# A recurrent token-mixing block on one core: zero matmuls ahead of the first transposes, the first batch's scaled rows taken from SBUF, and another written order

## The chip, the cores and the metric

The kernel runs on one core of one Trainium2 chip. Its engines work side by side, each on a queue of its own that it takes strictly in order: PE (TensorE, matrix products into PSUM), DVE (VectorE), ACT (ScalarE), POOL (GpSimd), and SP (SyncE), which here only issues DMAs. The metric is the device time of one execution in microseconds (us). Three runs of the kernel before took 615.41, 615.86 and 616.64 us; the median is 615.86 us.

## What is computed

One block of a recurrent network (RWKV-like) over x of shape 8 batches x 256 tokens x 512 channels, in float32, cut to what matters:

```python
xn = ln(x, ln1_w, ln1_b);  sx = shift(xn) - xn             # shift: the token before
xxx = tanh((xn + sx * maa_x) @ maa_w1).reshape(b, l, 5, 1, 32)
x5 = xn[:, :, None] + sx[:, :, None] * (maa_stack + xxx @ maa_w2)   # five mixes of each token
w = exp(-exp(time_decay + tanh(x5[:, :, 1] @ decay_w1) @ decay_w2))
r, k, v = x5[:, :, 3] @ Wr.T, x5[:, :, 0] @ Wk.T, x5[:, :, 2] @ Wv.T
g = silu(x5[:, :, 4] @ Wg.T)
# per head (32 heads of 16), token by token:
out = r @ (u * outer(k, v) + s);  s = outer(k, v) + w * s
att = groupnorm(out) * gn_w + gn_b
x = x + (att * g) @ Wo.T
xn2 = ln(x, ln2_w, ln2_b);  sx2 = shift(xn2) - xn2
x = x + sigmoid((xn2 + sx2*maa_r) @ Wr2.T) * (square(relu((xn2 + sx2*maa_k) @ Wk2.T)) @ Wv2.T)
```

## The kernel before

**Layout.** Between the two layer norms the activations lie with channels on the partitions: 512 channels are four blocks of 128, held as two tiles q = 0, 1 of two blocks m = 0, 1 each, with 256 tokens along the free axis. `normed` takes the statistics of the rows as they come from HBM (tokens on the partitions), scales them to `xh`, and `turned` turns them with eight transposes on PE (line 588) into PSUM tiles `ps`, from which `xn` is written with the norm's weight and bias.

**Stages.** For each of the 8 batches there are three: `inputs_of_scan` (norm, the mix `xin` with its product by `maa_w1` and the tanh `ta`, the products with `maa_w2`, called the psm products below, the five mixes `x5`, the decay, and the projections k, v, r, g), `scan`, and `rest` (group norm, output product, second norm, feed-forward). The stages of neighbouring batches run interleaved. The scan of a batch has 16 pieces: v is written to HBM as `vo` and read back in a spread layout as `vs`; DVE multiplies it by k (line 883), runs the recurrence with a scan instruction whose decay `wrep` lies in PSUM (line 885); POOL multiplies by r (line 888); PE sums over partitions (`gather`, line 896), four gathers a batch, 32 in all.

**The written order.** Every instruction group is an `Op` in a `Plan`. `TURNS` is a long string of numbers, one rank for each op and one list for each stage. `Plan.order` goes through the ops by rank, gives out buffers from the pools, computes a start for each op with a small model (`us` is an op's planned length), sorts by that start, and emits the instructions in that order. So ranks decide the order on every queue, which buffer a tile gets, and where an ACT function table has to be loaded again. `Plan.tiles` also decides from that order whether a product goes to PE as one 128-column matmul or as four of 32 columns that run side by side (`narrow` in `mul`, line 398); both take PE the same time. In the trace each float32 matmul is two records, a transpose one.

**The start.** Only for batch 0, `normed(..., alone=True, first=early)` is used: DVE does the statistics (line 554), ACT one square root (line 557), DVE the reciprocal and `xh` (lines 559 and 562). Then, for each block, two instructions read the same PSUM tile: DVE writes `xn` (line 595) and ACT writes the mix tile (line 598) as `ps * ow0 + ow1`. `owners` (line 517) prepares those two factors on POOL in four small instructions: ow0 = ln1_w (1 - maa_x) and ow1 = ln1_b (1 - maa_x). DVE then adds the shifted row times maa_x (line 622), POOL forms `sx` (line 610), and PE multiplies `xin` by `maa_w1`; between the transposes and these products PE has the `centered_weights` products (128x128, 16 of them) that subtract each head's mean from the v weights. `head_masks` (line 528) are four small DVE instructions that fill `hm`, needed later by the scan.

**The end.** The last batch's `rest` ends with the products `fk`, `fr`, `fv`; `fr` goes through a sigmoid on ACT (line 986), and the last token tile is written out in two halves.

Of the kernel before, what the change touches and what calls it, by code (L numbers as in the profile page):

```python
# [67 lines left out]
class Plan:  # L68
# [46 lines left out]
    def stage(self):  # L115
# [225 lines left out]
def tile_rwkv_block(  # L341
# [73 lines left out]
    dw1, dw2 = const("dw1", [P, NK, DEC]), const("dw2", [2 * DEC, E])  # L415
    hm = const("hm", [P, NK, 32])
    eh = const("eh", [P, 4])
    ow = const("ow", [P, 2, NK])
    W = {n: [const(f"W{n}{h}", [P, 2, E]) for h in range(2)] for n in "kvrg"}

    pool("s0", 2, [P, NK, S])
# [95 lines left out]
    def owners():  # L517
        i, j = (VECS.index(v) for v in ("maa_x", "ln1_w"))
        for n in range(2):
            gp(4, ow, [vec], lambda n=n: nc.gpsimd.tensor_tensor(  # L520
                ow()[:, n, :], vec()[:, :, j + n], vec()[:, :, i], ALU.mult), 30)
# [593 lines left out]
```

## Time and profile before

| what | value |
|---|---|
| median of three runs | 615.86 us (615.41 to 616.64) |
| the profiled execution's own time | 616.02 us |
| its span, first to last instruction | 614.2 us |
| matmul records in it | 7068 |
| HBM traffic | 115.25 MB read, 8.39 MB written |
| granted TensorE clock | 1.000 |

All durations below come from this one profiled execution. A row of the timeline has start and length in us, the engine, the line, the operation, the tiles, and in brackets how long the engine sat idle before it and what ended that. A row of the chain of waits has start, length, engine, tile and line; following the rows in order shows what the end of the span hung on at each time. A row of the table by stretches has the stretch, its length, and then the busy time of PE, PE's weight loads, DVE, ACT and POOL, with instruction counts. A busy PE row covers pipelined matmuls whose ends are modelled, so busy is not the same as full speed.

### The profile page before, as it was taken

How to read it: one execution, taken by the hardware profiler on the slowest of the kernel's cores; microseconds unless marked ns; L12 is line 12 of the kernel's file. 1: busy time of each engine (PE TensorE's matmuls, PEld its weight loads, DVE VectorE, ACT ScalarE, POOL GpSimd, SP SyncE). 2: the span in 40 equal slices, each digit the busy share in tenths (PEclk: the TensorE clock that was granted, in tenths of full speed). 3: DMA queues.
4: the chain of work that ended last, by engine and by line, in shares of the span. 5: the costliest groups of instructions: out<-in, count | busy, mean ns of one | idle time of the engine just before them, and what ended most of it. 6: DMA issues, size and time to landing. Idle time of an engine off the chain costs nothing.

```text
span 614.2 us, 17191 instructions
## 1 busy us (share of the span) xinstructions
PE 593.8 (97%) x7068; PEld 345.9 (56%) x7068; DVE 546.0 (89%) x487; ACT 515.8 (84%) x1171; POOL 522.3 (85%) x421
## 2 busy tenths in 40 slices
PE   4899999899999999999999999999999999999997
PEld 4575656457544764357653885465644474456463
DVE  5789999999999989799898999999999999995432
ACT  4878878999999989999999798999899799966431
POOL 2799999999989999899978999999969998897030
PEclk9999999999999999999999999999999999999999
DMA  8887779568969777867777896796958698681551
GB/s 291 272 199 184 194 186 257 141 176 211 273 174 255 188 187 211 212 201 208 221 188 221 269 230 181 179 273 166 246 142 221 174 257 233 203 238 36 195 186 46
DMA packets 52493, 124.73 MB, mean 203 GB/s; under 512 B 5824, under 2 KB 11200, under 8 KB 52416
## 3 DMA queue, kind: packets, MB, share of 16 engines
q1 hardware_dynamic: 48048, 119.46, 71.2%
q10 hardware_dynamic: 4368, 4.20, 2.2%
q8 instruction: 55, 0.90, 0.7%
q14 instruction: 22, 0.18, 0.1%
HBM read 115.25 MB, written 8.39 MB: 201 GB/s over the span
## 4 chain that ended last, share of the span: by engine, by line
PE 73%; ACT 13%; POOL 5%; DVE 4%; issue 2%; DMA 1%; ACTq 0%; SPq 0%; POOLq 0%; DVEq 0%
PE ps L401 61%; PE ps L896 8%; PE ps L588 2%; ACT att L846 1%; PE ps L760 1%; POOL st L888 1%; ACT wrep L866 1%; POOL mix L720 1%; ACT sq L951 1%; ACT rk L951 1%; DVE st L885 1%; DMA idt<-in_consts 1%; ACT vs L876 1%; ACT att L957 1%; ACT L866 1%
## 5 line engine op out<-in xcount | busy, mean ns | idle before, releaser
L885 DVE TENSOR_TENSOR_SCAN st<-wrep,vs 128x1024 f32<-128x1024 f32 x128 | 289.5, 2280 | 4.1 <-ACT wrep L866 1.0
L888 POOL TENSOR_TENSOR st<-st,r 128x1024 f32<-128x1024 f32 x128 | 254.4, 2001 | 6.2 <-DVE st L885 5.7
L883 DVE TENSOR_TENSOR vs<-vs,ps 128x1024 f32<-128x1024 f32 x122 | 144.2, 1207 | 2.4 <-ACT vs L876 2.1
L401 PE MATMUL ps<-Ws,mix 128*32 128x512 f32 (+1 forms) x864 | 115.0, 589 | 0.8 <-ACT o L986 0.8
L401 PEld LDWEIGHTS ps<-Ws,mix 128*32 128x32 f32 (+1 forms) x864 | 37.4, 116 | 64.8 <-issue 56.9
L720 POOL TENSOR_TENSOR mix<-mix,xn 128x512 f32<-128x512 f32 x62 | 66.7, 1090 | 7.6 <-DVE mix L705 7.6
L896 PE MATMUL ps<-st,con 128*32 128x256 f32 x1024 | 61.6, 380 | 0.9 <-POOL st L888 0.4
L401 PE MATMUL ps<-mix,Wv 128*32 128x256 f32 (+1 forms) x748 | 60.0, 380 | 0.3 <-DVE mix L717 0.3
L401 PE MATMUL ps<-mix,Wr 128*32 128x256 f32 (+1 forms) x616 | 59.2, 380 | 0.6 <-ACT vs L876 0.6
L401 PE MATMUL ps<-mix,Wk 128*32 128x256 f32 (+1 forms) x856 | 58.5, 380 | 0.5 <-DVE x L968 0.3
L401 PE MATMUL ps<-mix,Wg 128*32 128x256 f32 (+1 forms) x712 | 58.6, 379 | 0.0
L401 PE MATMUL ps<-mix,Ws 128*32 128x256 f32 (+1 forms) x688 | 58.0, 380 | 0.0
L401 PE MATMUL ps<-Ws,g 128*32 128x512 f32 (+1 forms) x416 | 56.6, 593 | 0.3 <-POOL g L962 0.2
L610 POOL TENSOR_TENSOR sx<-xn 128x512 f32<-128x512 f32 x31 | 32.3, 1052 | 27.5 <-ACT xn L605 22.5
L635 POOL TENSOR_TENSOR mix<-mix,xn 128x512 f32<-128x512 f32 x44 | 47.6, 1098 | 5.0 <-ACT mix L633 3.8
L846 ACT COPY att<-ps 32x256 f32<-32x256 f32 x128 | 46.7, 365 | 4.4 <-PE ps L838 2.3
L703 ACT ACTIVATE ps<-ps,vec 128x256 f32<-128x256 f32 x112 | 46.8, 443 | 4.1 <-PE ps L401 2.7
L401 PEld LDWEIGHTS ps<-mix,Wv 128*32 128x32 f32 (+1 forms) x748 | 40.2, 120 | 16.9 <-issue 2.3
L401 PEld LDWEIGHTS ps<-mix,Wr 128*32 128x32 f32 (+1 forms) x616 | 40.6, 128 | 16.1 <-POOL mix L720 1.1
L401 PEld LDWEIGHTS ps<-mix,Ws 128*32 128x32 f32 (+1 forms) x688 | 39.9, 123 | 16.1 <-ACT mix L633 0.8
L896 PEld LDWEIGHTS ps<-st,con 128*32 128x32 f32 x1024 | 32.5, 110 | 28.0 <-POOL st L888 4.7
L401 PEld LDWEIGHTS ps<-mix,Wg 128*32 128x32 f32 (+1 forms) x712 | 39.0, 122 | 15.6 <-issue 0.3
(133 smaller groups left out, 968.0 us busy)
## 6 DMA issues: line engine op xcount, KB each, us to landing
vs<-vo SPq DMA_DIRECT2D x128, 512.0 KB, 5.5
Ws<-in_wo SPq DMA_DIRECT2D x16, 512.0 KB, 5.3
Ws<-in_fr SPq DMA_DIRECT2D x16, 512.0 KB, 6.3
Ws<-in_fk SPq DMA_DIRECT2D x16, 512.0 KB, 7.2
Ws<-in_fv SPq DMA_DIRECT2D x16, 512.0 KB, 4.9
x<-in_x SPq DMA_DIRECT2D x9, 512.0 KB, 6.5
vo<-v ACTq DMA_DIRECT2D x15, 256.0 KB, 4.6
out<-o SPq DMA_DIRECT2D x15, 256.0 KB, 4.4
```

Of the source, the lines that this page charges most:

```text
L401: nc.tensor.matmul(out[i : i + n], lhsT=w[:, i : i + n], rhs=x, start=first, stop=final)
L588: nc.tensor.transpose(ps()[:, m, n * P : (n + 1) * P], xh[n]()[:, k * P : (k + 1) * P], idt())
L610: take(512, [sx], [xn], lambda xn=xn, sx=sx, e=nc.vector if quick else nc.gpsimd: e.tensor_tensor(sx(), xn()[:, :, 0:T], xn()[:, :, 1 : T ...
L635: gp(512, t, [t, xn[q]], lambda q=q, t=t: nc.gpsimd.tensor_tensor(t(), t(), xn[q]()[:, :, 1 : T + 1], ALU.add))
L703: act(256, p_, [p_, vec], lambda g=g, q=q, m=m, p_=p_: nc.scalar.activation(p_()[:, m, :], p_()[:, m, :], AF.Identity, bias=col(f"maa_{g}" ...
L720: gp(512, t, [t, xn[q]], lambda q=q, t=t: nc.gpsimd.tensor_tensor(t(), t(), xn[q]()[:, :, 1 : T + 1], ALU.add))
L846: act(350, atts[q], [pc], lambda i=32 * (2 * q + m), m=m, q=q, h=32 * h: nc.scalar.copy(atts[q]()[h : h + 32, m, :], pc()[i : i + 32, 0, :]))
L866: act(4 * T, w, [ew], lambda m=m, w=w, ew=ew: nc.scalar.activation(w()[:, :, 1:T], ew()[:, m : m + 1, 0 : T - 1].to_broadcast([P, 4, T - 1 ...
L883: dve(4 * T, [vs], [vs, kp], lambda m=m, vs=vs, kp=kp: nc.vector.tensor_tensor(vs(), vs(), kp()[:, m : m + 1, :].to_broadcast([P, 4, T]), ...
L885: dve(4 * T, [st], [w, vs], lambda w=w, vs=vs, st=st: nc.vector.tensor_tensor_scan(st().rearrange("p n t -> p (n t)"), w().rearrange("p n ...
L888: gp(4 * T, st, [st, r], lambda m=m, st=st, r=r: nc.gpsimd.tensor_tensor(st(), st(), r()[:, m : m + 1, :].to_broadcast([P, 4, T]), ALU.mul ...
L896: nc.tensor.matmul(pat()[32 * i : 32 * i + 32, 0, :], lhsT=con()[:, s : s + 32], rhs=done[i]()[:, j, :], start=(j == 0), stop=(j == 3),)
```

## The change

Four things change.

1. `warmed` is new: after a DVE memset of one half of the fourth `xn` buffer (`warm`, 128x257 elements), PE runs sixteen 128x256 matmuls of these zeros into a PSUM tile. It is the first entry on PE's queue, ahead of batch 0's transposes, and is planned with 5.8 us.
2. Batch 0's mix tile is no longer read from PSUM by ACT. ACT now reads `xn`, which DVE has just written to SBUF, and multiplies it by 1 - maa_x.
3. So `owners` has one POOL instruction in place of four, and `ow` is half as large.
4. `TURNS` is replaced as a whole. (`b > (1)` is the same as `b > 1`.)

```diff
@@ class Plan
     TURNS = """
-        5 50 8 34 35 59 43 77 41 122 129 94 125 138 20 21 22 23 145 146 152 153 18 2 26 19 38 57 32 39 58 31 33 56 44 60
...
@@ tile_rwkv_block
-    ow = const("ow", [P, 2, NK])
+    ow = const("ow", [P, NK])
...
+    warm = plan.pools["xn"][3][1]
+    nc.vector.memset(warm[:, 0, :], 0.0)
     nc.scalar.activation(plan.pools["mn"][1][1], eh()[:, 0:2], AF.Sqrt)
...
+    def warmed():
+        ps = new("ps", "psa")
+
+        def mm():
+            for n in range(16):
+                nc.tensor.matmul(ps()[:, 0, :], lhsT=warm[:, 0, 0:P], rhs=warm[:, 0, 0:T], start=True, stop=True)
+
+        pe(5.8, [ps], [], mm)
+
     def owners():
-        i, j = (VECS.index(v) for v in ("maa_x", "ln1_w"))
-        for n in range(2):
-            gp(4, ow, [vec], lambda n=n: nc.gpsimd.tensor_tensor(
-                ow()[:, n, :], vec()[:, :, j + n], vec()[:, :, i], ALU.mult), 30)
-        for n in range(2):
-            gp(4, ow, [vec, ow], lambda n=n: nc.gpsimd.tensor_tensor(
-                ow()[:, n, :], vec()[:, :, j + n], ow()[:, n, :], ALU.subtract), 30)
+        i = VECS.index("maa_x")
+        gp(4, ow, [vec], lambda: nc.gpsimd.tensor_scalar(ow(), vec()[:, :, i], -1.0, 1.0, ALU.mult, ALU.add), 30)
...
                     t = first[q]
-                    act(256, t, [ps, ow], lambda m=m, k=k, t=t, ps=ps: nc.scalar.activation(
-                        t()[:, m, :], ps()[:, m, :], AF.Identity,
-                        bias=ow()[:, 1, k : k + 1], scale=ow()[:, 0, k : k + 1]), pointers=2)
+                    act(256, t, [xn, ow], lambda m=m, k=k, t=t, xn=xn: nc.scalar.activation(
+                        t()[:, m, :], xn()[:, m, 1 : T + 1], AF.Copy, scale=ow()[:, k : k + 1]), pointers=1)
...
+    warmed()
     owners()
     head_masks()
     centered_weights()
```

What the new ranks do to the queues, read from the two programs' instruction lists: 22 of the 32 gathers stand after the same amount of PE work as before (the zeros not counted), the other ten moved by 0.4 to 5.2 us of PE work. ACT loads a function table 40 times instead of 43. On SP the identity for the transposes is issued before the first v weights instead of after them, and `vec` fifth instead of fourth. On DVE batch 0's four `xn` instructions go in the order q0 m0, q1 m0, q0 m1, q1 m1, with the four additions of the shifted rows (line 622) behind them, and the four `hm` instructions now stand in the middle of the mixes, ahead of the second half of the mix for k, where before they stood behind all mixes but the last group. On ACT the first two copies of the v weights stand ahead of `ta`'s table load as before (then three, now two), and behind `ta` the biases of the decay's mix (line 709) come before the second batch's `xh` (line 572), where before they alternated. Near the end, the sigmoids of the seventh batch stand behind the last batch's square root, and so share one table load with the last batch's own sigmoids.

More of the change, by code (lines that the diff above doesn't have):

```diff
@@ L538, in normed @@
             mn, nm = new("mn", f"mn{u}"), new("nm", f"nm{u}")
-        if (which == 1 and b > 1) or (which == 2 and b < 5):
+        if (which == 1 and b > (1)) or (which == 2 and b < 5):
             junk = [new("xh", f"xh{u}_{n}") for n in range(NT)]
```

238 rows, old and new, of the table TURNS are left out of this document.

## The prediction

> **What bounds the kernel now.** I read the page first (span, busy shares), then the busy time by stretches, then the timeline of the start and the end and the chain of waits.
>
> ```profile
> span 614.2 us, 17191 instructions
> ...
> PE 593.8 (97%) x7068; PEld 345.9 (56%) x7068; DVE 546.0 (89%) x487; ACT 515.8 (84%) x1171; POOL 522.3 (85%) x421
> ```
>
> ```profile
> 40.00:140.00 100.00, 95.86 (x1555) 57.04 (x1554) 98.46 (x81) 85.04 (x198) 99.38 (x70) 1.00 0.76 193
> 140.00:540.00 400.00, 398.11 (x4868) 226.02 (x4870) 383.62 (x307) 368.93 (x846) 369.01 (x289) 1.00 0.79 212
> 540.00:600.00 60.00, 59.42 (x359) 34.49 (x352) 33.63 (x47) 31.01 (x59) 29.73 (x25) 1.00 0.52 161
> ```
>
> Four stretches have different limits. Up to 40 us it is a chain of short steps over all engines. From 40 to 140 us POOL (99.38 of 100) and DVE (98.46) set the pace. From 140 to 540 us PE does (398.11 of 400). The end is PE with a few waits. So a gain in the first stretch moves everything behind it, by its own size at most; in the third a change can only remove or add waits of PE; and the matmuls themselves stay.
>
> Now the start, from the timeline and two stretches of PE alone:
>
> ```profile
> 0.80 0.06 DVE L463 MEMSET wrep<- 128x4 f32 x1 [0.80 <-PEq L1106]
> 5.47 1.00 DVE L562 TENSOR_SCALAR xh<-xt,mv,rs 128x512 f32<-128x512 f32 x2
> 7.25 1.94 PE L588 MATMUL ps<-idt,xh 128*128 128x128 f32 x8 [7.25 <-DMA idt<-in_consts]
> 7.69 0.35 POOL L523 TENSOR_TENSOR ow<-vec,ow 128x4 f32<-128x4 f32 x2
> 8.44 0.56 ACT L598 ACTIVATE mix<-ps,ow 128x256 f32<-128x256 f32 x1 [0.92 <-PE ps L588]
> 8.98 4.01 PE L401 MATMUL ps<-Ws,Ws 128*128 128x128 f32 x28
> 9.04 1.45 DVE L595 TENSOR_SCALAR xn<-ps,vec 128x256 f32<-128x256 f32 x3 [2.57 <-ACT mix L598]
> 10.07 1.48 ACT L598 ACTIVATE mix<-ps,ow 128x256 f32<-128x256 f32 x3 [0.98 <-DVE xn L595]
> 11.69 1.56 ACT L514 COPY Wv<-ps 128x512 f32<-128x512 f32 x3
> 12.04 1.66 DVE L622 SCALAR_TENSOR_TENSOR mix<-xn,vec,mix 128x256 f32<-128x256 f32 x2
> 12.21 2.39 POOL L610 TENSOR_TENSOR sx<-xn 128x512 f32<-128x512 f32 x2 [4.17 <-DVE xn L595]
> 14.23 0.65 DVE L622 SCALAR_TENSOR_TENSOR mix<-xn,vec,mix 128x256 f32<-128x256 f32 x1
> 14.94 0.70 PE L401 MATMUL ps<-mix,mw 128*128 128x256 f32 x2 [0.48 <-DVE mix L622]
> 15.67 0.39 ACT L680 ACTIVATE ta<-ps 128x256 f32<-128x256 f32 x1 [1.11 <-PE ps L401]
> 19.00 1.09 PE L588 MATMUL ps<-idt,xh 128*128 128x128 f32 x8 [0.89 <-ACT xh L572]
> ```
>
> ```profile
> 7.20:10.50 3.30, 3.25 (x16) 1.00 0.99 347
> 10.50:12.80 2.30, 2.30 (x22) 1.00 1.08 370
> ```
>
> ```profile
> 435.14 1.73 PE ps L401 x8
> ```
>
> Three things to see. The transposes wait for a DMA (the identity, 7.2 us), not for `xh`, ready at 6.47. ACT and DVE take turns at the PSUM tile: each row says it waited for the other. And PE is slow at first: 16 records in 3.25 us up to 10.5, then 22 in 2.3, although the clock column says 1.00 in both; the eight transposes cost 1.94 us here and 1.09 at 19.0. So PE ran at half speed for its first 3.25 us of work.
>
> **The zeros.** They start when DVE has cleared the buffer. The trace has only a clear of 4 columns (0.06 us from 0.80); I take 0.3 us for 257 and 0.1 for the handover, so PE starts near 1.3. Sixteen float32 matmuls of 256 columns are 32 records. Warm, a record takes 1.73 / 8 = 0.216 us; at half speed 0.43. If PE again needs 3.25 us, 7.6 records go in that time and the other 24.4 take 5.3: the zeros end at 1.3 + 3.25 + 5.3 = 9.8 us. That is later than the 7.25 at which the transposes start now, so they hold up the very work they warm PE for, by 2.6 us. Even warm from the first record they would end at 1.3 + 6.9 = 8.2 (lower bound). Upper bound: PE needs twice 3.25 us, 15 records in 6.5 us and 17 warm ones in 3.7, so 11.5. I take 9.8, since the trace's one warm-up is the nearest row.
>
> The Trainium skill, "TensorE: Matmul & The Clock Gate", section "Part 1: The HAM clock gate", says that the array's clock is gated to half until one window of about 3.4 us has been busy, and that this window is free-running; worked out, the flip can then come as late as two windows after PE starts. The 3.25 us seen here agrees with one; by the late case of the rule the zeros would end at about 11.6 us as an estimate, and the whole change would then come out near no change.
>
> **From the transposes to `ta`.** Let T be the transposes' start. Before, T = 7.25 and `ta` starts at 15.67, 8.4 later. Cold transposes hand the first tile to ACT 1.2 us after their start (8.44); warm ones should take 0.7. So after, DVE writes the four `xn` pieces without waiting for ACT, 0.5 us each (1.45 for three), to T + 2.7. ACT follows from SBUF.
>
> ```profile
> L633 ACT ACTIVATE mix<-sx,vec 128x256 f32<-128x256 f32 x88 | 40.4, 500 | 2.6 <-POOL sx L610 2.0 <-DVE sx L610 0.4
> ```
>
> A row of this form (SBUF to SBUF, one scale) takes 0.50 us against 0.56 for line 598, so ACT ends half a microsecond behind DVE, and DVE's additions (line 622) can start at T + 2.9. One should take about 0.5, as line 595 does, but the two at 12.04 took 1.66 and ended only after POOL's first `sx`: while POOL reads two SBUF tiles, this kind of DVE instruction waits. POOL now has `sx` from T + 2.3 to T + 4.6, right over them. Free of that they would end at T + 4.8; if they wait out both, at T + 5.7. I take 5.7. Then 0.8 us for the last products with `maa_w1`, as from 14.88 to 15.67 now: `ta` at T + 6.5 = 16.3, 0.6 us later than now (between 14.7 and 18.0 for T of 8.2 and 11.5). PE is no limit there: warm centering products take 28 x 0.105 = 2.9 us in place of 4.0. ACT's two weight copies (0.52 each by the row of three) and its table load (1.28, the row quoted for the end) end before `ta` has its input. The three POOL instructions saved in `owners` were done by 8.0 us and cost nothing now, because `ow` is first read at 8.44.
>
> **From `ta` to the first scan.**
>
> ```profile
> 19.21 0.83 ACT L709 ACTIVATE mix<-wrep,vec 128x256 f32<-128x256 f32 x2
> 19.39 2.96 POOL L711 TENSOR_TENSOR mix<-mix,sx 128x512 f32<-128x512 f32 x2 [2.35 <-ACT mix L709]
> 22.31 4.22 POOL L720 TENSOR_TENSOR mix<-mix,xn 128x512 f32<-128x512 f32 x4
> 24.41 2.17 DVE L528 TENSOR_SCALAR hm<-con,vec 128x32 f32<-128x32 f32 x2
> 26.59 1.93 PE L401 MATMUL ps<-mix,Wk 128*32 128x256 f32 x32 [0.16 <-POOL mix L720]
> 30.93 1.13 DVE hm L528
> 33.26 0.72 ACT w L783 x2
> 34.57 0.91 ACT wrep L866
> 38.12 1.96 POOL st L888
> ```
>
> POOL starts at 19.39, 3.7 us behind `ta`, on ACT's biases. After, ACT has `ta` itself (0.39), two copies (1.04), a small instruction and two biases (0.83) ahead of POOL's first piece, 2.3 us and the small one: I take 2.7, a gain of 1.0 for the decay's mix. The k mix loses it again. An `hm` instruction has 32 columns and yet takes 1.1 us, and the two from 24.41 end at 26.58, with POOL's at 26.53: DVE waits for POOL here too. The new order puts all four ahead of the second half of the k mix, for which POOL and then PE's k product wait. Two of them find POOL busy (2.2 us); the others find it idle, waiting for that very mix, and should be short. So the k product, now 10.9 us behind `ta`, stays there. But no `hm` stands at 30.93 any more, where the chain runs through it between the k product and `wrep`; behind the k copy come the two decay pieces (0.72) and `wrep` (0.91) without that 1.1. So the first scan, and the POOL product now at 38.12, come 1.0 us sooner behind `ta`. If `hm` took its 1.1 us all four times, 2.2 more stand on the k path and the gain turns into a loss of 1.2. DMAs: the new order of SP's first loads brings the identity sooner and `vec` one place later, but both are needed only from T on. Sum of the first stretch: +0.6 - 1.0 = **-0.4 us** (from -2.0 at T = 8.2 to +1.3 at T = 11.5). From 40 to 140 us POOL and DVE do the same instructions, so it passes through.
>
> **The new order in the middle.** PE's work is the same but for the zeros, and the gathers stand where they stood, 22 of 32 exactly. What differs is how much PE work lies between a product and the one that needs its result.
>
> ```profile
> 50.53 1.15 PE L401 MATMUL ps<-ta,mw2a 32*128 32x256 f32 x16 [0.53 <-DVE mix L705]
> 245.33 1.15 PE L401 MATMUL ps<-ta,mw2a 32*128 32x256 f32 x16 [0.42 <-ACT o L986]
> 256.01 1.15 PE L401 MATMUL ps<-ta,mw2a 32*128 32x256 f32 x16 [0.81 <-DVE o L1009]
> ```
>
> Between the `maa_w1` product and the first psm product lie, batch by batch, 0.4, 1.7, 14.2, 3.4, 3.4, 3.5, 3.4, 9.0 us before and 0.4, 1.7, 17.7, 3.9, 6.9, 1.7, 1.7, 8.6 after. The fifth batch's psm products, at 245.33 and 256.01, wait 0.42 and 0.81 now and get twice the room: up to 1.2 gained. The sixth and seventh go down to 1.7, with which the second waits 0.53 at 50.53: up to 1.1 lost. These cancel. PE's idle time in the third stretch is 400 - 398.1 = 1.9 us, and that is all that waits can give there; three new ones of the larger kind would cost 2.4. I take **-0.2 us** (-1.9 to +3).
>
> **The end.**
>
> ```profile
> 602.61 1.28 ACT L986 ACT_TABLE_LOAD   x1 [5.64 <-PE ps L401]
> 603.90 1.08 ACT L986 ACTIVATE o<-ps 128x512 f32<-128x512 f32 x2
> 605.04 5.44 PE L401 MATMUL ps<-Ws,mix 128*128 128x256 f32 x20 [0.78 <-ACT o L986]
> ```
>
> Here PE stops 0.78 us for a PSUM tile that the last sigmoid has to leave, and that sigmoid waits for its table. After, the table is in place from the seventh batch's sigmoids, and PE has the whole other token tile (four 512-column products, 3.4 us) ahead of the tile it must wait for. Gain **0.8 us** (none, if ACT comes late for another reason; 1.3, the whole load, if more hangs on it).
>
> **Sum.** -0.4 - 0.2 - 0.8 = -1.4 us against this execution's span of 614.2 us, so 612.8. Its own time was 616.02, 0.16 above the median, and the 1.8 around the span stay; from the median, 615.86 - 1.4 = 614.5 us.
>
> **Rivals.**
> (1) The change loses at its head because PE does not warm on zeros. All 32 records at 0.43 are 13.8 us, T = 15.1, `ta` at 21.6 or later: +5.9 in place of +0.6, in all 615.86 + 3.9 = 619.8. It decides from T = 11.2 on, where the sum is zero. For it: zeros switch nothing, and the trace has no matmul of zeros. Against: the half speed ended 3.25 us after PE's first work, through transposes and weight products alike; nothing in the trace ties it to the values.
> (2) The head is neutral, but waits appear in PE's own stretch because psm products were drawn nearer to their inputs. Four or five of the 0.81 us kind: +3.6, in all 615.86 - 1.2 + 3.6 = 618.3. It decides from two such waits. For it: the two leads cut to 1.7 us. Against: most of the order stands.
> (3) Nothing measurable: T late by a window (11.5) or the gain of the head given back in the 40 to 140 stretch, where a DMA or an `hm` wait takes its place: 615.2 to 616.3.
> (4) PE is warm at once and the waits at 245 and 256 go: -2.0 - 1.2 - 0.8 = -4.0, 611.9; with a better 40 to 140 stretch 610.
>
> **How the numbers follow.** Forecast (612.5 to 614.6) 0.41; rival (4) 0.10; rival (3) 0.21; rival (2) 0.19; rival (1) 0.09. What a measurement can tell from no change is 0.2%, 1.2 us. Faster: 0.41 + 0.10 = 0.51; within: 0.21; slower: 0.19 + 0.09 = 0.28. The forecast's own range, with each term halfway to its bounds (-3.3 to +1.4), is 612.5 to 617.3; to hold 8 in 10, with the fast rival and most of the slow ones in, it becomes 610.5 to 619.0.
>
> **What would show it.** In the profile after: the zeros' 32 records from about 1.3 to 9.8 us, the first third of them at 0.43; transposes of 1.1 us starting at 9.8 and not at 7.2; no waits between lines 595 and 598 in turn, but the additions of line 622 stretched beside POOL's `sx`; `ta` near 16.3; four `hm` instructions, two short; the first product with r on POOL near 37.7; no table load and no PE wait behind 600 us; PE's idle time from 140 to 540 us near 2 us. The forecast is wrong if transposes start before 8.5 or behind 11, or if PE idles over 4 us in the third stretch.

## The result, and the profile after

The changed kernel takes 619.32 us in the median of four runs (618.49 to 619.56), the kernel before, beside it, 615.77 (615.41 to 616.64). The ratio is 1.0053, 95% interval 1.0036 to 1.0071: it is slower, where 614.5 and a small gain were forecast. The profiled execution took 619.48 us with a span of 617.7, 3.5 more than the span before.

From the page of the changed kernel:

```profile
span 617.7 us, 17520 instructions
...
PE 603.2 (98%) x7232; PEld 353.3 (57%) x7232; DVE 544.5 (88%) x488; ACT 512.3 (83%) x1168; POOL 522.1 (85%) x418
```

The table by stretches of the changed kernel (start:end, length, busy time of PE, its loads, DVE, ACT, POOL):

```profile
40.00:140.00 100.00, 96.94 (x1558) 57.58 (x1557) 98.18 (x82) 85.61 (x199) 99.41 (x69) 1.00 0.77 199
140.00:540.00 400.00, 396.39 (x4982) 226.41 (x4984) 381.20 (x306) 369.07 (x844) 366.90 (x287) 1.00 0.77 211
540.00:600.00 60.00, 59.15 (x384) 33.47 (x377) 37.39 (x49) 28.37 (x60) 33.17 (x28) 1.00 0.45 146
```

PE's idle time from 140 to 540 us rose from 1.9 to 3.6 us. Where the 3.5 us came from is seen better by following one kind of event through both traces: the first scan, then the gathers (PE's 32 groups with `con`), then the end. Changed kernel less kernel before: +1.0 us at the first scan, +2.1 at the gather at 501 us, +3.9 at the one at 533 and at the last, +3.5 at the end. So there are two losses of about 1, a step of 1.8 within 30 us, and 0.4 given back at the end.

The timeline of the start, changed kernel:

```profile
1.17 9.63 PE L523 MATMUL ps<-xn 128*128 128x256 f32 x32 [1.17 <-DVE xn L461]
6.09 1.00 DVE L567 TENSOR_SCALAR xh<-xt,mv,rs 128x512 f32<-128x512 f32 x2
10.63 1.04 PE L593 MATMUL ps<-idt,xh 128*128 128x128 f32 x8
11.27 1.90 DVE L600 TENSOR_SCALAR xn<-ps,vec 128x256 f32<-128x256 f32 x4 [4.18 <-PE ps L593]
11.92 1.80 ACT L603 ACTIVATE mix<-xn,ow 128x256 f32<-128x256 f32 x4 [4.07 <-DVE xn L600]
12.88 2.22 POOL L614 TENSOR_TENSOR sx<-xn 128x512 f32<-128x512 f32 x2 [5.07 <-ACT mix L603]
13.08 3.08 DVE L626 SCALAR_TENSOR_TENSOR mix<-xn,vec,mix 128x256 f32<-128x256 f32 x4
17.03 0.38 ACT L684 ACTIVATE ta<-ps 128x256 f32<-128x256 f32 x1 [0.71 <-PE ps L400]
23.19 0.85 DVE L533 TENSOR_SCALAR hm<-con,vec 128x32 f32<-128x32 f32 x1
24.35 1.15 DVE L533 TENSOR_SCALAR hm<-con,vec 128x32 f32<-128x32 f32 x3
28.29 1.93 PE L400 MATMUL ps<-mix,Wk 128*32 128x256 f32 x32 [0.19 <-POOL mix L724]
36.56 2.29 DVE L889 TENSOR_TENSOR_SCAN st<-wrep,vs 128x1024 f32<-128x1024 f32 x1
```

and the first scan of the kernel before:

```profile
35.53 2.29 DVE L885 TENSOR_TENSOR_SCAN st<-wrep,vs 128x1024 f32<-128x1024 f32 x1
```

`xh` is complete at 7.09 and waits 3.5 us for the zeros: the transposes start at 10.63. From there the picture is the one forecast: transposes at full speed (1.04 us in place of 1.94), DVE and ACT writing their four pieces without taking turns, `ta` 6.4 us behind the transposes instead of 8.4. That buys back 2.0 of the 3.4 us; what follows `ta` gives 0.3 more.

### The profile page after: what moved, and what is told of

It is laid out like the page before. It is cut to its first block, busy times and chain, and to the rows that moved or that the text cites. A ratio compares the mean times of both kernels' runs of the same rounds, so it can differ in the third digit from the quotient of the medians.

```text
span 617.7 us, 17520 instructions
## 1 busy us (share of the span) xinstructions
PE 603.2 (98%) x7232; PEld 353.3 (57%) x7232; DVE 544.5 (88%) x488; ACT 512.3 (83%) x1168; POOL 522.1 (85%) x418
## 4 chain that ended last, share of the span: by engine, by line
PE 72%; POOL 13%; ACT 7%; DVE 5%; issue 3%; DVEq 0%; POOLq 0%; ACTq 0%
PE ps L400 59%; PE ps L900 7%; POOL st L892 5%; POOL mix L724 3%; PE ps L593 2%; PE ps L523 2%; POOL vs L884 1%; PE ps L764 1%; DVE st L889 1%; ACT rk L955 1%; ACT mix L637 1%; POOL mix L752 1%; ACT L931 1%; ACT att L961 1%; ACT sq L955 1%
## 5 line engine op out<-in xcount | busy, mean ns | idle before, releaser
L400 PE MATMUL ps<-Ws,mix 128*32 128x512 f32 (+2 forms) x864 | 115.6, 589 | 0.3 <-ACT o L990 0.3
L900 PE MATMUL ps<-st,con 128*32 128x256 f32 x1024 | 62.3, 381 | 1.5 <-ACT r L795 0.9
L900 PEld LDWEIGHTS ps<-st,con 128*32 128x32 f32 x1024 | 32.9, 110 | 28.9 <-issue 5.5
```

The lines of the kernel that those rows point to most:

```text
L400: nc.tensor.matmul(out[i : i + n], lhsT=w[:, i : i + n], rhs=x, start=first, stop=final)
L900: nc.tensor.matmul(pat()[32 * i : 32 * i + 32, 0, :], lhsT=con()[:, s : s + 32], rhs=done[i]()[:, j, :], start=(j == 0), stop=(j == 3),)
```

## The experiments

Every kernel below does the whole computation. Besides the number of zeros and the place from which ACT reads, what varies is the order: "old turns" means that each op of the changed kernel has its rank from the kernel before, so that every queue stands as before. T is the start of the transposes; T, `ta` and the first scan are of the profiled execution; the time is the median of the runs in us, and a ratio compares a kernel with runs of the kernel before taken beside it.

| run | zeros | ACT reads | turns | T | ta - T | first scan | median (range) | ratio to before, 95% |
|---|---|---|---|---|---|---|---|---|
| before | 0 | PSUM | old | 7.25 | 8.42 | 35.53 | 615.86 (615.41 to 616.64) | |
| e1_before_z8 | 8 | PSUM | old | 7.11 | 8.08 | 35.07 | 616.12 (615.63 to 616.96) | 0.9994 to 1.0012 |
| e1_before_z16 | 16 | PSUM | old | 11.20 | 7.93 | 39.01 | 619.37 (618.33 to 619.52) | 1.0039 to 1.0064 |
| e3_old_turns_z0 | 0 | SBUF | old | 7.08 | 7.90 | 34.66 | 616.06 (614.68 to 616.45) | 0.9989 to 1.0006 |
| e4_old_turns_z6 | 6 | SBUF | old | 7.17 | 6.95 | 33.79 | 614.40 (614.02 to 614.89) | 0.9966 to 0.9984 |
| e2_old_turns_z8 | 8 | SBUF | old | 7.64 | 6.63 | 33.94 | 614.19 (613.66 to 614.96) | 0.9962 to 0.9983 |
| e2_old_turns | 16 | SBUF | old | 9.75 | 6.63 | 36.05 | 617.34 (616.55 to 618.00) | 1.0016 to 1.0036 |
| e1_after_z0 | 0 | SBUF | new | 6.66 | 7.98 | 34.16 | 617.57 (617.10 to 618.27) | 1.0017 to 1.0035 |
| e1_after_z8 | 8 | SBUF | new | 7.54 | 6.40 | 33.48 | 616.73 (616.55 to 620.12) | 1.0007 to 1.0032 |
| after | 16 | SBUF | new | 10.63 | 6.39 | 36.56 | 619.32 (618.49 to 619.56) | 1.0036 to 1.0071 |
| e4_psum | 16 | PSUM | new | 9.79 | 6.66 | 36.48 | 620.02 (619.54 to 620.61) | 1.0054 to 1.0079 |

### The zeros alone

```diff
-            for n in range(16):
+            for n in range(0):          # e1_after_z0; range(8) in e1_after_z8
                 nc.tensor.matmul(ps()[:, 0, :], lhsT=warm[:, 0, 0:P], rhs=warm[:, 0, 0:T], start=True, stop=True)
```

> The changed kernel without its sixteen matmuls of zeros; every other instruction keeps its place. Theory A (the zeros run past the point where xh is ready and so hold up the head; the new turns cost the rest behind 140 us): the transposes start when xh is there (about 7.1 us, 3.5 sooner than in the changed kernel) but at half speed, ta near 15.0 (1.9 to 2.4 sooner than 17.03), first scan 1.5 to 2.5 us sooner, whole time 617.0 to 618.0: still above the kernel before. Theory B (the zeros alone make the loss, the new turns are neutral): 615.0 to 616.0. Theory C (what the head gains is swallowed by POOL and DVE between 40 and 140 us): head 2 us sooner, end unchanged, 619.0 to 619.6.

> The changed kernel with eight matmuls of zeros (16 records of 256 columns) in place of sixteen; order as in the changed kernel. At 0.427 us for the first 12 records and 0.216 for the next 4 the zeros end about 7.2 us, as xh gets ready. Theory A: transposes warm from 7.2 us, ta near 13.7 (3.3 sooner), first scan near 33.2, whole time 616.0 to 616.6, the best of the four with the new turns. Theory B: 614.0 to 615.0. Theory C: 618.5 to 619.6. If the end of the half speed depends on a clock that runs by itself and not on when the work began, the sixteen records may take up to 6.9 us (end 8.0).

In the kernel before, put in ahead of everything:

```diff
+    warm, cold = plan.pools["xn"][3][1], plan.pools["ps"][0][1]
+    nc.vector.memset(warm[:, 0, :], 0.0)
+    for _ in range(16):                 # range(8) in e1_before_z8
+        nc.tensor.matmul(cold[:, 0, :], lhsT=warm[:, 0, 0:P], rhs=warm[:, 0, 0:T], start=True, stop=True)
```

> The kernel before, its order untouched, with the sixteen matmuls of zeros put in front. Theory A: the zeros end near 10.8 us, transposes 3.4 us later than in the kernel before, partly paid back by warm transposes and centering products (1.9 us): ta 1.0 to 1.5 us later, whole time 616.8 to 617.5. Theory B (zeros make the whole loss of 3.5): 619.0 to 619.6. If the zeros cost nothing: 615.4 to 616.2.

> The kernel before, its order untouched, with eight matmuls of zeros in front. Theory A: zeros end about 7.2 us, where the identity lands and the transposes start anyway; these then run in 1.1 us, not 1.94, and the centering products in 2.9 us, not 4.0: ta 0.8 to 1.8 us sooner (13.9 to 14.9), whole time 614.0 to 615.0. Theory C (40 to 140 us swallows it): 615.4 to 616.0.

Without zeros the changed kernel still takes 617.57, 1.7 above the kernel before: the zeros are not the whole loss, and the 1.75 us between the two medians are theirs (2.4 between the two profiled executions, where the half speed's end differs). With eight it is 616.73, just above theory A's range. The two runs on the kernel before went against theory A. Sixteen zeros alone cost 3.5 us there, as much as the whole change; and eight, which end before the transposes could start anyway, gain nothing that can be measured. Theory C is not the reason for that: the first scan is only 0.5 us sooner, and those 0.5 stand unchanged at the last gather. The timeline of the kernel before with eight zeros says why:

```profile
1.17 5.92 PE L464 MATMUL ps<-xn 128*128 128x256 f32 x16 [1.17 <-DVE xn L462]
7.11 1.06 PE L592 MATMUL ps<-idt,xh 128*128 128x128 f32 x8
8.57 1.45 DVE L599 TENSOR_SCALAR xn<-ps,vec 128x256 f32<-128x256 f32 x3 [2.12 <-ACT mix L602]
9.60 1.48 ACT L602 ACTIVATE mix<-ps,ow 128x256 f32<-128x256 f32 x3 [0.98 <-DVE xn L599]
15.19 0.38 ACT L684 ACTIVATE ta<-ps 128x256 f32<-128x256 f32 x1 [1.37 <-PE ps L401]
```

PE is twice as fast, but DVE and ACT still wait for each other at the PSUM tile (2.12 and 0.98 us in the brackets), and that sets `ta`. A faster PE is worth 0.34 us in `ta` - T there.

### The read from SBUF, and the turns

For the old turns the ranks of the kernel before were put in for the same ops, with the zeros first:

```diff
     TURNS = """
-        3 55 7 16 24 81 53 62 82 60 35 91 86 85 14 13 88 95 96 97 6 5 15 29 32 51 27 57 63 28 30 48 26 34 64,
+        6 48 9 32 33 57 41 75 39 120 127 92 123 136 0 21 143 144 150 151 19 3 24 20 36 55 30 37 56 29 31 54 42 58 69,
...
```

> The whole change but for the new turns: sixteen matmuls of zeros, the scaled rows read from SBUF, and the turns of the kernel before (every engine in its old order). Theory A (three separate prices: zeros +3.5 as in the kernel before with sixteen zeros, SBUF read a gain in the head, new turns a loss behind the head): first scan 1.0 to 2.5 us later than in the kernel before and the same delay to the end, 617.0 to 618.4, below the changed kernel. Theory D (the SBUF read gives nothing; the head's gain in the changed kernel against the kernel before with sixteen zeros comes from the new turns): first scan 3.5 later, 619.0 to 619.6. Theory E (the new turns are a gain that hides something worse in the SBUF read): over 619.6.

> As the run with the old turns, but eight zeros in place of sixteen. Theory A: the first scan 1.0 to 2.1 us sooner than in the kernel before, carried to the end unchanged: 613.8 to 615.0, faster than the kernel before. Theory D: 615.4 to 616.2, as the kernel before with eight zeros. Theory C (the stretch from 40 to 140 us swallows a gain of the head): the first scan sooner, the end unchanged, 615.6 to 616.2.

> Old turns, scaled rows read from SBUF, no zeros: the SBUF read alone. Theory A (the read pays because ScalarE and VectorE no longer take turns at the PSUM tile, and pays less while PE is at half speed): first scan 0 to 0.8 us sooner than in the kernel before, 615.0 to 615.9; the new turns without zeros (617.57) then cost 1.7 to 2.5. If the read pays the same 1.6 us with a cold PE: 614.0 to 614.6, and the zeros are worth nothing. If it pays only because of the zeros: 615.6 to 616.2.

Theory A held for both runs with zeros; the run without them, 616.06, falls into the range of "only because of the zeros". In each run with zeros the shift of the first scan against the kernel before (+0.5 and -1.6 us) stands to within 0.1 at all 32 gathers and at the end. So a gain or loss in the head is worth its full size in these runs, and the old turns lose none of it. Between equal numbers of zeros the new turns cost 617.57 - 616.06 = 1.5 us without zeros, 2.5 with eight and 2.0 with sixteen. And the read from SBUF, with old turns: 616.12 to 614.19 with eight zeros, 619.37 to 617.34 with sixteen, 1.9 and 2.0 us; without zeros nothing in the median. With sixteen zeros the parts add up: +3.5 for the zeros, -2.0 for the read and +2.0 for the turns make the 3.5 of the whole change. The medians also hold how long the half speed happened to last. Counted from T to the first scan in the profiled executions, which leaves that out, the read is worth 1.7 us with eight zeros, 1.5 with sixteen and 0.7 with none. In the run without zeros the first scan is 0.9 us sooner in the profiled execution, but two waits of PE near 315 and 336 us, which the kernel before does not have, take 0.65 back, and 0.4 more goes after 520. The runs of that kernel reach down to 614.7. Why it loses this stays open.

From the timeline of the old turns with eight zeros, the same place as above:

```profile
7.64 1.04 PE L497 MATMUL ps<-idt,xh 128*128 128x128 f32 x8
8.28 1.45 DVE L504 TENSOR_SCALAR xn<-ps,vec 128x256 f32<-128x256 f32 x3 [1.73 <-PE ps L497]
9.42 0.90 ACT L507 ACTIVATE mix<-xn,ow 128x256 f32<-128x256 f32 x2
14.27 0.38 ACT L588 ACTIVATE ta<-ps 128x256 f32<-128x256 f32 x1
```

DVE now waits for PE's transposes, not for ACT. So most of the gain needs both edits: `ta` - T is 8.42 with neither, 8.08 with zeros alone, 7.90 with the SBUF read alone, 6.63 with both.

The reverse test undoes the SBUF read in the changed kernel:

```diff
...                     # ow and owners as in the kernel before
-                    act(256, t, [xn, ow], lambda m=m, k=k, t=t, xn=xn: nc.scalar.activation(
-                        t()[:, m, :], xn()[:, m, 1 : T + 1], AF.Copy, scale=ow()[:, k : k + 1]), pointers=1)
+                    act(256, t, [ps, ow], lambda m=m, k=k, t=t, ps=ps: nc.scalar.activation(
+                        t()[:, m, :], ps()[:, m, :], AF.Identity,
+                        bias=ow()[:, 1, k : k + 1], scale=ow()[:, 0, k : k + 1]), pointers=2)
```

> The changed kernel with the SBUF read undone: ScalarE takes the scaled rows from the PSUM tile again (with its scale and bias, and the four small instructions on GpSimd); order unchanged, sixteen zeros stay. Theory A (the read pays about 1.6 us, since VectorE and ScalarE take turns at the tile without it): first scan 1.0 to 1.8 us later than in the changed kernel, 620.2 to 621.2. Theory D (the read gives nothing): 619.0 to 619.7.

It came out between the theories, 0.7 us above the changed kernel, and the two intervals overlap. In the new order DVE writes two pieces from two PSUM tiles before it needs one that ACT reads, so there is less turn-taking to remove: `ta` - T is 6.66 against 6.39. That is 0.3 of the 0.7. The rest cannot be given to the read, since something else differed too: in the profiled execution of e4_psum the granted clock was 0.91 from 20 to 40 us, where it was 1.00 in the changed kernel. Four transposes there took 1.06 us in place of 0.60, and the first scan came 0.5 later behind `ta`.

### Where the new turns lose

The step between 501 and 533 us, first in PE's timeline, kernel before and changed kernel (L896 and L900 are the gathers):

```profile
501.14 1.93 PE L896 MATMUL ps<-st,con 128*32 128x256 f32 x32
...
518.83 1.91 PE L896 MATMUL ps<-st,con 128*32 128x256 f32 x32
...
533.05 1.92 PE L896 MATMUL ps<-st,con 128*32 128x256 f32 x32
```

```profile
503.27 1.93 PE L900 MATMUL ps<-st,con 128*32 128x256 f32 x32
...
507.18 1.91 PE L400 MATMUL ps<-mix,Wr 128*32 128x256 f32 x32
509.30 1.93 PE L400 MATMUL ps<-mix,Wk 128*32 128x256 f32 x32 [0.21 <-ACT sq L931]
...
521.38 1.91 PE L900 MATMUL ps<-st,con 128*32 128x256 f32 x32
523.11 1.90 PE L400 MATMUL ps<-Ws,mix 128*32 128x512 f32 x16
525.33 1.93 PE L400 MATMUL ps<-mix,Ws 128*32 128x256 f32 x32 [0.33 <-issue]
527.86 5.39 PE L400 MATMUL ps<-mix,Ws 128*32 128x256 f32 x96 [0.59 <-ACT o L990]
...
536.93 1.91 PE L900 MATMUL ps<-st,con 128*32 128x256 f32 x32
```

In the changed kernel PE waits three times, at 509.30, 525.33 and 527.86; in the kernel before it does not wait in this stretch. Where nothing waits, the next group starts 1.73 us after such a group. By the starts of the rows the three waits therefore cost 0.4, 0.5 and 0.8 us, which together are the step. The brackets name ACT for the first (the square root's result `sq`) and for the third (the sigmoid's `o`); for the second the profile names no cause.

Then ACT in the same two kernels:

```profile
491.59 0.38 ACT L768 ACTIVATE tb<-ps 64x256 f32<-64x256 f32 x1
494.26 0.38 ACT L768 ACTIVATE tb<-ps 64x256 f32<-64x256 f32 x1
504.47 1.28 ACT L927 ACT_TABLE_LOAD   x1
512.81 1.28 ACT L866 ACT_TABLE_LOAD   x1
520.27 1.28 ACT L986 ACT_TABLE_LOAD   x1
529.06 1.03 ACT L866 ACTIVATE wrep<-w 128x1020 f32<-128x1020 f32 x1
```

```profile
492.73 0.78 ACT L770 ACTIVATE w<-ps 64x256 f32<-64x256 f32 x2 [2.50 <-PE ps L764]
505.73 0.64 ACT L918 ACTIVATE sq<-att 128x512 f32<-128x512 f32 x1 [1.08 <-DVE att L906]
507.48 1.28 ACT L931 ACT_TABLE_LOAD   x1 [1.11 <-PE ps L926]
510.45 1.28 ACT L772 ACT_TABLE_LOAD   x1
511.75 0.77 ACT L772 ACTIVATE tb<-ps 64x256 f32<-64x256 f32 x2
525.92 1.28 ACT L990 ACT_TABLE_LOAD   x1
532.87 1.03 ACT L870 ACTIVATE wrep<-w 128x1020 f32<-128x1020 f32 x1
```

From the square root's load (504.47 and 507.48) to the `wrep` ACT pauses for 1.0 and 0.2 us in all, so here ACT hardly rests. Ahead of it, from 488 us on, ACT stands idle in the changed kernel (2.50, 1.08 and 1.11 us; in the kernel before at most 0.85 at a time), and inside it are the two `tb` (0.77 us) that were done before it in the old order. The sigmoid's table comes 5.65 us later, and PE, which needs the tile that the sigmoid leaves, stops. Five tables are loaded in the stretch in both: it is not their number. To test that the step belongs to the order of this part, both orders were cut at rank 2100 (near 470 us) and joined (given here as the rule by which the numbers of `TURNS` were made, as in the later pieces of this kind):

```diff
-rank(op) = new(op)
+rank(op) = new(op) if new(op) < 2100, behind them the others by old(op)     # e2_late_old, 16 zeros
+rank(op) = old(op) if old(op) < 2100, behind them the others by new(op)     # e3_late_new_z8, 8 zeros
```

> The changed kernel up to about 470 us; behind that the turns of the kernel before. Theory A (the new order of ScalarE between 505 and 535 us, with the table load for the sigmoid behind eight copies and two loads of exp, costs 1.8 us; the new end saves 0.4 to 0.8): the delay of the gathers stays at 2.1 from 500 to 561 us in place of 3.9, the stop of PE near 603 us is back, 617.8 to 618.3. Rival (the loss of that stretch is a transfer or a clock effect and not the order): 619.2 to 620.2.

> Old turns with SBUF read and eight zeros up to about 470 us, behind that the new turns. Theory A (the stretch from 505 to 535 us costs 1.8 by ScalarE's new order, the new end gives back 0.4 to 0.8): the delay of the gathers steps up by 1.5 to 2.5 us there, 615.2 to 616.2 against 614.19 with old turns throughout. Rival (the stretch costs only behind a late head): 613.4 to 614.3.

Both show it. With the old late order the delay of the gathers is 2.2 to 2.3 us from 473 to 561 us, without the step, and the median is 618.77, a little above what theory A said. With the new late order alone the delay is -1.5 until 460, -0.9 from 473 to 501, and +0.9 from 533 on; the median rises from 614.19 to 616.37, 2.2 us and likewise a little above theory A, though the head is early, so the rival (only behind a late head) falls. The joint itself costs 0.6 in each. PE's three waits go with the order as well: of 0.21, 0.33 to 0.34 and 0.58 to 0.59 us, they stand in the profiled executions of all five kernels that have the new order there (the changed kernel, e1_after_z0, e1_after_z8, e4_psum, e3_late_new_z8), and in none of the kernel before, e2_old_turns_z8 and e2_late_old.

Which engine's order makes the step was to be told by giving the late part of ACT one order and that of TensorE and the DMA queue the other:

```diff
+late op on ACT: rank by old, every other late op by new                     # e4_late_act_old
+late op on ACT: rank by new, every other late op by old                     # e4_late_act_new
```

> Old turns, SBUF read, eight zeros up to about 470 us; behind that TensorE, the DMA queue and, but for a few lines, VectorE and GpSimd in the new order, ScalarE in the old one. Theory A (ScalarE's new order makes the step of 1.8 us between 505 and 535): no such step, 613.6 to 614.8. Rival (the new order of TensorE makes it, ScalarE only waits for it): the step stays, 615.6 to 616.6. Two orders that do not fit each other may wait for one another: over 617.

> The reverse: behind about 470 us TensorE and the DMA queue in the old order, ScalarE in the new one. Theory A: the step of 1.5 to 2.5 us between 505 and 535 is there, 615.6 to 616.8. Rival (TensorE's order makes it): no step, 613.8 to 614.6.

Neither told it: 633.80 and 630.75 us. The two orders wait for one another; in each the delay grows by 17 to 18 us between 460 and 561 us. The step belongs to the new late order as a whole, and it is made of PE's three waits; that ACT's moved `tb` and its idle time bring these about is a reading of the trace and was not shown.

The other loss of the new turns, 1.1 us between the first scan and 501 us, is spread wider: against the first scan it is 0.2 to 0.3 by 180 us, 0.8 by 320 and 1.1 by 460, in the changed kernel with sixteen zeros and with none. Its largest part, 0.5, falls between the gathers at 223 and 250 us, where PE has a wait at 248.12 (0.32 us, shown further below) that the kernel before does not have. No run divides it further.

### Toward a faster kernel

One run kept the new turns at the start (ranks below 250) and at the end (from 2400 on), old ones between:

> The changed kernel with eight zeros, and with the new turns only in the first 80 and the last 70 us or so; between them the turns of the kernel before. Theory A: head 2.1 sooner, nothing lost in between, 0.4 to 0.8 more gained at the end: span 611.3 to 612.0, 612.8 to 613.8. If the old turns in between cost as much with a sooner head: 615.0 to 616.7.

It missed theory A: 615.10 us. Its profiled execution is the slowest of its twelve runs (617.02; the granted clock was 0.81 and 0.85 in the 5 us before and after 20 us), so its trace shows where that run lost, and not the median one. In it the first scan is 1.8 us early, and at the third `wrep` it is 0.5 late: 2.3 go at the first joint, in part perhaps by the clock. From 98 to 519 us the delay stays at 0.2, so the old turns in between lose nothing. Another 1.2 go at the second joint near the end.

Fewer zeros, and the identity loaded one place earlier on SP:

```diff
-SP: xt, xt, Ws, idt, vec
+SP: xt, xt, idt, Ws, vec            # e3_idt_z6 (range(6)) and e3_idt_z8 (range(8)); e4_old_turns_z6 without this move
```

> Old turns, SBUF read, six matmuls of zeros (12 records), and the identity's load moved one place forward in SyncE's queue. Zeros end between 5.6 and 6.5 us, so the transposes start with the first half of xh (6.7), 0.9 sooner than with eight zeros (7.64). Theory A: first scan 2.0 to 2.5 us sooner than in the kernel before, 613.2 to 613.8. Where the half speed lasts longer than the zeros, some transposes and centering products run cold, and up to 0.8 of it is lost (614.0 to 614.6).

> As the run with six zeros and the identity moved, but eight zeros. Transposes start at 6.7 to 7.7 us, as the half speed ends early or late: first scan 1.6 to 2.4 sooner, 613.4 to 614.3. The identity was not late with eight zeros, so little or nothing against the same without the move (614.19).

> Old turns, SBUF read, six zeros, the identity's load in its old place. Zeros end between 5.1 and 6.5 us; the transposes wait for the identity (7.1). Theory A: as with eight zeros, or 0.3 sooner where the half speed ends late: 613.7 to 614.4. If PE falls back to half speed in the pause of 0.6 to 2 us before the identity lands: 615.4 to 616.2, as without zeros.

With the identity early, the transposes do start at 6.60, but `ta` comes 7.03 us behind (6.95 with six zeros and no move, 6.63 with eight), and the scan 0.6 later behind `ta`: 614.30 us, above theory A and no better than eight zeros without the move. One reason stands in the trace of e3_idt_z6. DVE's first `xn` needs the norm's weight and bias in `vec`, and these land only at 7.3 us:

```profile
7.38 1.45 DVE L504 TENSOR_SCALAR xn<-ps,vec 128x256 f32<-128x256 f32 x3 [0.83 <-DMA vec<-in_vecs]
```

So `vec` is the next thing that the head waits for behind the identity, though it explains only 0.1 us here (DVE starts 0.78 us behind T and not 0.64). Why `ta` and the scan lose the rest stays open. With eight zeros the profiled execution was the best of its runs (613.85) and the median 615.02, above its forecast, with single runs up to 616.82. Much of that scatter lies outside the span: the spans go from 611.8 to 613.3, and the time around them from 1.8 to 3.6 us, where it is 1.7 to 1.9 in the kernel before. What makes it is not explained. Six zeros without the move give 614.40: six and eight cannot be told apart.

Last, the new end alone behind the old turns, eight zeros and the SBUF read, with the cut at rank 2520 and at 2560:

> Old turns, SBUF read, eight zeros, and the new turns in the last batch's end alone (from its silu pieces and square root on): the sigmoid's table is in place before the last token tile. Theory A (the stop of PE for that table, 0.8 us, goes; nothing else changes): the delay of the last gather as with old turns (-1.6), the tail 0.4 to 0.8 shorter, 613.3 to 613.8. If ScalarE's moved pieces hold up PE there: 614.2 to 615.5.

> The same with the new turns from about 20 us later on (from the seventh batch's last sigmoid): the table for the square root is loaded between the two sigmoids, so one load more than in the other run, where ScalarE waits anyway. Theory A: 613.3 to 613.9. If the table load between them holds up the seventh batch's output: 614.2 to 615.0.

```diff
+rank(op) = old(op) if old(op) < 2520 (2560 in e5_new_end_late), behind them the others by new(op)
```

They take 614.29 (613.67 to 614.68) and 613.84 us (613.23 to 614.72), with ratios to the kernel before (616.33 beside these two) of 0.9949 to 0.9976 and 0.9943 to 0.9973; the first lies above its theory A, the second within. PE's last groups with the old end (e2_old_turns_z8) and with the second of these:

```profile
603.40 5.44 PE L304 MATMUL ps<-Ws,mix 128*128 128x256 f32 x20 [0.79 <-ACT o L894]
```

```profile
593.38 13.92 PE L304 MATMUL ps<-Ws,mix 128*128 128x512 f32 x40
```

The stop of 0.79 us is gone in both. From the last gather to the end it is 53.2 us with the old end, 52.8 in e5_new_end, as in the changed kernel, and 52.1 in e5_new_end_late. e2_old_turns_z8, e5_new_end and e5_new_end_late all beat both the kernel before and the changed one; among themselves their intervals overlap, so what the new end adds to the old turns is seen in the tail of the traces, not in the medians.

## Why the prediction was wrong

**What bounds the kernel.** Right: a gain or loss of the head passes through at full size, shown by the runs with old turns.

**The zeros.** The mechanism was right, that the zeros hold up the transposes; the term was too small. T was put at 9.8 and is 10.63, inside the bounds (8.2 to 11.5). The row taken for the warm-up, 3.25 us, is one draw, and in the changed kernel's profiled execution the half speed lasted 5.0 us: with sixteen zeros T is 9.75 to 11.20 in the profiled executions of five kernels, according to when the half speed ends.

**From the transposes to `ta`.** Right: 6.4 us against 6.5, with DVE's additions beside POOL's `sx` (3.08 us for four: two of 1.12 and 1.25 beside it, then two of 0.47), no turn-taking, and transposes of 1.04 us. What the prediction did not say is that most of this gain comes only with both edits together.

**From `ta` to the first scan.** The gain of 1.0 was 0.3. The `hm` instructions were as forecast (two of 0.85 beside POOL's work, two of 0.23), but the k product starts 11.26 us behind `ta`, not 10.9, and the way from it to the first scan became 0.7 shorter, not 1.1. Head in all: -0.4 forecast, +1.0 measured.

**The new order in the middle.** This step failed. It was put at -0.2 us (-1.9 to +3) by counting how much PE work lies between the `maa_w1` product and the psm product that needs its result. That lead decided nothing:

```profile
246.66 1.15 PE L400 MATMUL ps<-ta,mw2a 32*128 32x256 f32 x16 [0.52 <-ACT o L990]
248.12 3.64 PE L400 MATMUL ps<-Ws,mix 128*32 128x512 f32 x32 [0.32 <-ACT o L990]
...
257.76 1.15 PE L400 MATMUL ps<-ta,mw2a 32*128 32x256 f32 x16 [0.80 <-DVE o L1013]
```

The first and the last row are the two waits that were to go with twice the room, in the changed kernel: 0.52 and 0.80 us, where they were 0.42 and 0.81. The brackets name the instructions on `o` and not `ta`, and the quoted rows of before had said so. The two leads that were cut to 1.7 us did no harm either: behind 258 us no psm product waits 0.1 us for `ta`. What was measured is +2.9 from the first scan to the last gather. Of that, 1.8 are PE's three waits between 501 and 533 us, two of them for ACT; the prediction did not look at that stretch, since it took 140 to 540 us as one stretch bound by PE. Another 0.5 falls around the row at 248.12, a new wait for `o`. Rival (2), waits in PE's own stretch, is nearest in kind, but the waits are not for the inputs of psm products, and its 618.3 keeps the head's -0.4 although it calls the head neutral.

**The end.** -0.8 forecast, -0.4 measured, and the stop is gone as forecast. The last part of the new end alone, behind the old turns (e5_new_end_late), gave -1.1.

**The sum**: +1.4 in the head, +3.1 in the middle and +0.4 at the end make up the difference between -1.4 and +3.5. Of the rivals, (1) falls: zeros do bring full speed. Its 619.8 is the nearest of all numbers, by luck. (4) falls too, since PE was not warm at once and both waits stayed.

## What to carry to other kernels

Warming matmuls are free only until the operand of the work behind them is there: here, with the same order and the SBUF read, eight come out 1.9 us below none, and sixteen 1.3 above. Ask first whether PE is what the head waits for; here it became that only when ACT and DVE stopped taking turns at one PSUM tile. And a new written order is better priced stretch by stretch than by the bound of the whole: PE is 98% busy here, and yet the largest single loss behind the head lies in 30 us in which it waits three times, twice for ACT. That a count by ACT would have forecast it was not tried.

## What the hardware showed beside this

**When the half speed ends.** In the first 10 us the clock column says 1.00 in every profile, but the records of the zeros show it: 0.427 us apart, then 0.216. The same zeros, started at 1.17 us each time, in two more kernels:

```profile
1.17 8.78 PE L523 MATMUL ps<-xn 128*128 128x256 f32 x32 [1.17 <-DVE xn L461]
```

```profile
1.17 10.19 PE L464 MATMUL ps<-xn 128*128 128x256 f32 x32 [1.17 <-DVE xn L462]
```

(e4_psum and e1_before_z16; the changed kernel's 9.63 stands above.) Over the 17 profiled executions with zeros, the starts of single records put the change of speed between 3.0 and 6.1 us after PE's first work, spread over the whole of that. In the kernel before it came after 3.25. The Trainium skill, "TensorE: Matmul & The Clock Gate", section "Part 1: The HAM clock gate", says that the window of about 3.4 us runs freely and has to be busy once; worked out, that gives 3.4 to 6.8 us after the start. The traces agree in kind, with a spread as wide as one window, but not in the figure: in five of the 17 the change came by 3.3 us, and the measurement decides. A window of about 3.05 us is an estimate from the two ends of the spread.

**A pause did not cost the speed.** In e4_old_turns_z6 PE stood still for 1.33 us between the last zeros and the transposes, and these still ran 0.109 us apart behind the first.

**The granted clock dipped in two profiled executions.** It was 0.66 from 20 to 25 us in e4_psum, and 0.81 and 0.85 from 15 to 20 and 20 to 25 us in e2_mix_z8; in the other 18 it read 1.00 over the first 60 us. What sets it off is not shown.
